# A four-layer graph network on one core: more row gathers by TensorE and SyncE in three stages

## The chip, the cores and the metric

The kernel runs on one core of one Trainium2 chip. The metric is the device time of one execution in microseconds (us).

## The reference

A graph has 12,500 nodes with 64 features and 400,000 edges, sorted by target `dst`. Four layers follow each other, each ending in x = layernorm(x + layer(x)).

```python
# layer 0: max over a node's incoming edges of W2 relu(W1 [x_dst, x_src - x_dst])
# layer 1: mean of edge_attr over a node's outgoing edges, then a two-layer network on [x, mean, u]
# layer 2: mean of x[src] over incoming edges, a gate of three groups, a linear map
msg_sum = segment_sum(feature[src], dst)
h = msg_sum / max(deg, 1)
# layer 3: attention over incoming edges; weights by type of node (4) and of edge (8), 4 heads of 16
k, q, v = (typed_linear(x, W, node_type) for W in (Wk, Wq, Wv))
a = (typed_head(k[src], rel_att, etype) * typed_head(q[dst], rel_att, etype)).sum(-1) * pri / 4
m = typed_head(v[src], rel_msg, etype)
h = segment_sum(m * softmax_over_dst(a), dst)
out = typed_linear(h, Wa, node_type)
```

## The kernel before, in words

Edges lie on chip as 128 lanes (partitions) of 3125 consecutive edges. A *tile* is one edge of each lane, so 128 rows; a *group* is 25 tiles. There are 124 such groups, and the last 25 tiles are cut into three short groups of 16, 8 and 1. Nodes are 98 tiles of 128. The program is unrolled and runs stage after stage: sorting of places, the scatter of layer 1's rows by source (L768), layers 0 and 1 over edges, a node stage, layer 2 over edges, a node stage, layer 3 over edges, a node stage.

Rows that depend on an index are fetched by GpSimd, one indirect DMA a tile (`gather`, L214): in layer 2 rows of 64 from X2 into `gx`, in layer 3 rows of 128 (keys and values, worked out in the node stage for each of 8 edge types) from TKM into `gk`. The scatter writes rows of 65 from `at` to SRT in the same way.

Some tiles are fetched otherwise. `row_by_row` (L237 to L245) loads 32 addresses into registers and issues one small DMA a row, from SyncE (SP) or ScalarE (ACT): two tiles in two groups of five in layer 2 (`ROWS2`), one tile in every third group (`single`) of layer 3 (`ROWS3`). In layer 2 two tiles a group (`PE2`) come from TensorE: x is on chip as three bf16 parts (`part`). The source number is split into a block (`key_b`) and a place among 13 x 128 columns (`keys`). A matmul spreads the keys over partitions (`pk`, L1208), DVE compares them with `own` to get a one-hot `hot` of 128 x 1664 (L1212), and 39 matmuls (13 chunks by three parts, 128 x 512, the last chunk's three 128 x 128) give the rows of eight blocks in `pr` (L1218). `take` picks the right block by `hb`, a multiply `one` (L1230) and a sum (L1231).

Each group then needs a running sum or maximum along the lane. Layer 2 has a chain of 25 scalar_tensor_tensor instructions (L1251). A layer-3 step spreads q along the lane (`st`, 25 instructions, L1419), multiplies it with the keys in five pieces and adds up (`pr`, `sc`, L1426, L1427), takes a running maximum `M` (L1434), differences `ex`, exponentials on ACT (L1442, L1443), a running denominator `L` (L1446), the weighted values `wm` (four pieces, L1454) and one long scan `hs` (L1459). ACT copies `hs`, `M` and `L` into `R`, which SP stores.

Queues: a DMA issued by SP stands in program order behind what SP issued before. In layer 3 SP's order is written out by hand, and that of the other engines is a scheduler's; in the scatter and in layer 2 SP, ACT, PE and DVE are ordered by hand. `gk` and `st` have three buffers, `gx` five, `at` four, `pr` of layer 2 four.

Of the kernel before, what the change touches and what calls it, by code (L numbers as in the profile page):

```python
# [9 lines left out]
F32 = mybir.dt.float32  # L10
BF = mybir.dt.bfloat16
# [8 lines left out]
P = 128  # L20
D = 64
# [23 lines left out]
ROWS2 = 5, (1, 3)  # L45
PE2 = 2
NC = 13
ROWS3 = 3
RL = 32
ZC = 200  # L50


@with_exitstack
def resnorm_gnn_kernel(ctx: ExitStack, tc: tile.TileContext, a: dict, out: bass.AP):
# [21 lines left out]

    const = ctx.enter_context(tc.tile_pool(name="const", bufs=1))
    to_l2 = ExitStack()
    to_l0 = ExitStack()
# [304 lines left out]

    xs = const.tile([P, NT, D], F32, name="xs")
    if NREM:
# [285 lines left out]
    def turned(k):  # L672

        if k >= len(rounds):
            return
        m, w = rounds[k][2], work[k]
        oh, ol = w["hots"]
        pT = ups.tile([NT, 4, P], F32, name="pT")
        for j in range(m):
            nc.tensor.matmul(pT[:, j, :], oh[:, j, :], identh, start=True, stop=True)  # L680
        pH = ups.tile([NT, 2, P], F32, name="pH")
        for s, n in ((0, min(2, m)), (1, m)):
            for j in range(n):
                nc.tensor.matmul(pH[:, s, :], oh[:, j, :], ol[:, j, :], start=(j == 0), stop=(j == n - 1))
        w["hT"] = hT = up.tile([NT, 4, P], HF, name="hT", bufs=3)
        nc.scalar.activation(hT[:, :m, :], pT[:, :m, :], AF.Copy)
        H = up.tile([NT, P], F32, name="H", bufs=3)
        nc.vector.tensor_add(H, now[0], pH[:, 1, :])
        now[0] = H
        if m > 2:  # L690

            w["then"] = B = up.tile([NT, P], HF, name="then", bufs=3)
            nc.vector.scalar_tensor_tensor(B, pH[:, 0, :], 1.0 / U8, w["tables"][1], op0=ALU.mult, op1=ALU.add)
# [46 lines left out]
    now = [begin]  # L740
    todo = [0]

    def advance():

        k = todo[0]
        hot(k + 2)
        turned(k + 1)
        ol = work[k]["hots"][1]
        pG = spots(k)
        if k + 2 in work:  # L750
            work[k + 2]["tables"] = tables(now[0])
        pairs(k + 1)
        sums_of(k, pG, ol)
        todo[0] += 1

# [8 lines left out]
    def scatter(i, between=()):  # L764
        at, _, to = placed.pop(i)
        for j in range(G):

# [7 lines left out]
            if j % 4 == 0 and between:  # L775
# [3 lines left out]
                puts0.append(row)  # L779
        return put  # L780

# [64 lines left out]
    keep = const.tile([P, EP], F32, name="keep")  # L846
    negm = const.tile([P, EP], F32, name="negm")
    w64 = const.tile([D, P], F32, name="w64")
# [81 lines left out]
    def carry_over(psp, sb, last):  # L930

        ps = psp.tile([D, P], F32, name="ps_c")
        nc.tensor.transpose(ps, last, ident)  # L933
        return ps
# [208 lines left out]
    to_n1.close()  # L1143


    with tc.tile_pool(name="e2", bufs=2) as sb, tc.tile_pool(name="e2ps", bufs=1, space=PSUM) as psp:
        pm = sb.tile([P, D], F32, name="m2", bufs=1)
# [5 lines left out]
        for k, g in enumerate(single):  # L1153
            at = groups[g][0] + G - 2
            nc.vector.tensor_copy(cols[:, k, :], srcS[:, at : at + 2])
        places = places_of(psp, sb, cols.rearrange("p k t -> p (k t)"), 4 * D, "places")
        at, n3 = groups[3][0] + G - 1, len(range(3, NG - 1, ROWS3))
        assert n3 <= P
        places3 = places_of(psp, const, stS[:, at : at + (n3 - 1) * ROWS3 * G + 1 : ROWS3 * G], 8 * D, "places3")
        X2b = bytes_of(X2)  # L1160
# [10 lines left out]
        for b in range(NBA):  # L1171
            t = slice(b * NB, (b + 1) * NB)
            rest = xs[:, t, :]
            for k in range(3):
                nc.scalar.activation(parts[k][:, t, :], rest, AF.Copy)
                if k < 2:
                    left = sb.tile([P, NB, D], F32, name=f"left{k}")
                    nc.vector.tensor_sub(left, rest, parts[k][:, t, :])
                    rest = left
        own = sb.tile([P, NC], F32, name="own", bufs=1)  # L1180
        nc.vector.tensor_scalar(own, frow[:, :NC], float(P), pcol, op0=ALU.mult, op1=ALU.add)
        by_pe = slice(G - 2 - PE2, G - 2)
        dense = range(2, NG - 1)
        n = len(dense) * PE2
        keys = sb.tile([P, n], HF, name="keys", bufs=1)
# [3 lines left out]
        with tc.tile_pool(name="e2k", bufs=1) as ksb:  # L1189
            num = ksb.tile([P, n], I32, name="num")  # L1190
            at = groups[dense[0]][0]
            nc.vector.tensor_copy(num.rearrange("p (g t) -> p g t", t=PE2),
                                  srcS[:, at : at + len(dense) * G].rearrange("p (g t) -> p g t", t=G)[:, :, by_pe])
            part_i = ksb.tile([P, 3, n], I32, name="part_i")
# [6 lines left out]

        def by_one_hots(g):


            k = (g - dense[0]) * PE2
            pk = psp.tile([P, PE2, P], F32, name="pk", bufs=1)
            for j in range(PE2):
                nc.tensor.matmul(pk[:, j, :], keys[:, k + j : k + j + 1].to_broadcast([P, P]), identh, start=True, stop=True)  # L1208
            got = []
            for j in range(PE2):  # L1210
                hot = sb.tile([P, NC, P], BF, name="hot", bufs=4)
                nc.vector.tensor_tensor(hot, pk[:, j, None, :].to_broadcast([P, NC, P]),  # L1212
                                        own[:, :, None].to_broadcast([P, NC, P]), ALU.is_equal)
                pr = psp.tile([P, 8, D], F32, name="pr", bufs=4)
                for c in range(NC):
# [5 lines left out]
                got.append(pr)  # L1221
            return k, got

        def take(got, gx):
            k, got = got
            for j, pr in enumerate(got):
                hb = sb.tile([P, 8], F32, name="hb", bufs=4)
                nc.vector.tensor_scalar(hb, eight, key_b[:, k + j : k + j + 1], None, op0=ALU.is_equal)
                one = sb.tile([P, 8, D], F32, name="one")
                nc.vector.tensor_mul(one, pr, hb[:, :, None].to_broadcast([P, 8, D]))  # L1230
                nc.vector.tensor_reduce(gx[:, by_pe.start + j, :], one.rearrange("p b f -> p f b"), AX.X, ALU.add)  # L1231

        ahead = {}
        with tc.manual_schedule(engines={SP, ACT, mybir.EngineType.PE, mybir.EngineType.DVE}):
            for g, (c0, ng) in enumerate(groups):
                if g + 2 in dense:
                    ahead[g + 2] = by_one_hots(g + 2)
                if g + 2 in single:
# [4 lines left out]
                gx = tiles_of(g)  # L1243
                if g in ahead:
                    take(ahead.pop(g), gx)
                mine = [j for j in range(ng) if not (g in single and j >= G - 2 or g in dense and by_pe.start <= j < by_pe.stop)]
                for j in mine:
# [8 lines left out]
        row = ends_of_lanes(sb, R2, D)  # L1256
        ps = carry_over(psp, sb, pm)
        u = sb.tile([D, P], F32, name="u2", bufs=1)
        nc.vector.tensor_tensor_scan(u, w64, ps, 0.0, ALU.mult, ALU.add)
        nc.vector.tensor_add(row, row, shifted(psp, sb, u, "g2"))  # L1260
        put_ends(R2, row)

    to_l2.close()

    def types_of(t, t0, nt):
# [24 lines left out]
    with tc.tile_pool(name="n2", bufs=1) as sb, tc.tile_pool(name="n2ps", bufs=2, space=PSUM) as psp:  # L1290
        puts = []

        def nodes2(b, t0, nt):
# [65 lines left out]
            for j in range(nt):  # L1359
# [18 lines left out]
                )  # L1378
                yield

        in_turn(nodes2, [1, 2, 4] + [NB] * (NBA - 1), lambda n: n + 1,
                {getattr(mybir.EngineType, e) for e in ('PE', 'Activation', 'DVE', 'SP')})


    with tc.tile_pool(name="e3", bufs=2) as sb, tc.tile_pool(name="e3ps", bufs=1, space=PSUM) as psp:
        pa = sb.tile([P, D], F32, name="a3", bufs=1)
# [25 lines left out]
        def step(g, c0, ng):  # L1412
            nonlocal pa, M, L, hs, last, R
            gk, st = keys_of(g), sts.pop(g)
            for j in range(ng - (g in single)):
                gather(gk[:, j, :], TKM, stS[:, c0 + j : c0 + j + 1])
            for j in range(ng):
# [5 lines left out]
            for q in range(0, ng, 5):  # L1423
# [4 lines left out]
                                        pr.rearrange("p c (h d) -> p c h d", d=HS), AX.X, ALU.add)  # L1428
            nm = negm[:, c0 : c0 + ng]
            Mp, Lp, hp = M, L, hs  # L1430
# [9 lines left out]

            weight = psp.tile([P, NH, ng], F32, name="weight", bufs=2)
            nc.scalar.activation(weight, ex[:, 1, :, 1:], AF.Exp)  # L1442
# [33 lines left out]
        R = None  # L1476
        with tc.manual_schedule(engines={SP}):
            load_starts(0)
            load_starts(1)
            for g, (c0, ng) in enumerate(groups):  # L1480
                step(g, c0, ng)

        row = ends_of_lanes(sb, R3, W3)
# [42 lines left out]
    with tc.tile_pool(name="n3", bufs=1) as sb, tc.tile_pool(name="n3ps", bufs=2, space=PSUM) as psp:  # L1526
        def nodes3(b, t0, nt):
# [28 lines left out]
            y = tile_of([P, nt, D], "y")  # L1556
            nc.vector.tensor_add(y, po, xs[:, cols, :])
            o = tile_of([P, nt, D], "o")
# [38 lines left out]
```

## Time and profile before

| what | us |
|---|---|
| median of 3 runs (lowest, highest) | 16245.76 (16243.42, 16247.37) |
| profiled execution | 16243.81 |
| its span | 16242.0 |
| GpSimd busy | 12210.0 |
| DVE busy | 10664.7 |
| PE busy | 7545.9 |
| ACT busy | 2681.6 |
| scatter, first to last indirect write (L768) | 1266.7 to 5379.7 |
| layer 2, first to last gather | 8409.2 to 11892.6 |
| layer 3, first to last gather | 12191.5 to 16056.8 |

Busy time says what an engine did, not what it waited for. GpSimd's busy time leaves out the issue of its DMAs, about 0.3 us after each. A view by stretch gives busy times, the granted TensorE clock (1.00 is full) and the DMA share of any interval; the timeline gives single instructions with the idle time before them and what ended it. Line numbers in the profile are those of the kernel before.

### The profile page before, as it was taken

Reading aid. Unit: us, or ns where it says so; the run is one execution under the profiler, and the core shown is the slowest. Engines: PE = TensorE matmul, PEld = TensorE weight load, DVE = VectorE, ACT = ScalarE, POOL = GpSimd, SP = SyncE. Lnnn points to the kernel's source line nnn. Section 1 sums busy time; section 2 is a strip of 40 time slices with the busy share of each in tenths; the row PEclk is TensorE's granted clock in tenths of the full one; section 3 lists DMA queues with packets and bytes.
Section 4 is the critical chain, followed back from the end, with each engine's and each line's share of the span. In section 5 each row is a group of like instructions: output and inputs, shape, how many; then the busy total and the mean of one; then the engine's idle time right before and its main releaser. Section 6 shows DMA issues by size and latency. Waiting matters only on the chain. (4 is left out here: it accounts for less than half of the span.)

```text
span 16242.0 us, 201759 instructions
## 1 busy us (share of the span) xinstructions
PE 7545.9 (46%) x52153; PEld 5379.1 (33%) x52153; DVE 10664.7 (66%) x29306; ACT 2681.6 (17%) x5002; POOL 12210.0 (75%) x12724
## 2 busy tenths in 40 slices
PE   4455666666654566666546666666660000000002
PEld 4444555554543455555522222222240000000002
DVE  9996777777774577777445555555545666666666
ACT  0012333333322011111120000000031212212222
POOL 7777777777777777777767777777767777777776
PEclk6667777777776677777768888888885555555555
DMA  3333233222222465656312222222253333333333
GB/s 78 120 107 90 84 86 86 69 52 54 54 52 52 154 206 195 203 200 205 114 41 56 58 59 56 57 58 59 58 180 110 109 109 109 113 106 111 112 109 97
DMA packets 1130450, 1634.82 MB, mean 101 GB/s; under 512 B 755218, under 2 KB 760850, under 8 KB 1128898
## 3 DMA queue, kind: packets, MB, share of 16 engines
q1 hardware_dynamic: 684322, 1093.23, 20.1%
q0 software_dynamic: 406880, 520.58, 13.1%
q10 hardware_dynamic: 38080, 8.06, 0.2%
q8 instruction: 414, 6.78, 0.2%
q14 instruction: 754, 6.18, 0.1%
HBM read 883.71 MB, written 737.15 MB: 100 GB/s over the span
## 5 line engine op out<-in xcount | busy, mean ns | idle before, releaser
L768 POOL DMA_INDIRECT SRT<-at,to x3125 | 3036.9, 972 | 952.5 <-issue 946.7
L214 POOL DMA_INDIRECT gk<-TKM,stS x3084 | 2926.2, 949 | 940.3 <-issue 922.3
L214 POOL DMA_INDIRECT gx<-X,srcS x2783 | 2635.2, 947 | 875.3 <-issue 791.0
L1218 PE MATMUL pr<-part,hot 128*128 128x512 bf16 (+1 forms) x9516 | 2229.7, 401 | 1176.0 <-DVE one L1230 1150.1
L214 POOL DMA_INDIRECT gb<-TB,srcS x2125 | 2073.1, 976 | 647.6 <-issue 624.5
L1251 DVE SCALAR_TENSOR_TENSOR gx<-gx,keep 128x64 f32<-128x64 f32 x3124 | 892.6, 286 | 1463.2 <-DMA gx<-X,srcS 1226.7
L933 PE MATMUL ps_c<-ident,full 128*64 128x128 f32 x3 | 1.3, 420 | 3900.4 <-DVE full L1486 3898.9
L1218 PEld LDWEIGHTS <-hot 128*128 128x128 bf16 x9516 | 975.2, 105 | 2430.5 <-DVE hot L1212 858.0
L1066 DVE SCALAR_TENSOR_TENSOR R<-R,negm,msg 128x64 f32<-128x64 f32 x3124 | 858.0, 275 | 820.5 <-PE msg L997 816.2
L933 PEld LDWEIGHTS ps_c<-ident,full 128*64 128x64 f32 x3 | 0.4, 128 | 3901.8 <-DVE full L1486 3899.7
L214 POOL DMA_INDIRECT xg<-in_x,srcS x1000 | 953.6, 954 | 306.2 <-issue 296.6
L1426 DVE TENSOR_TENSOR pr<-st,gk 128x320 f32<-128x320 f32 x627 | 306.8, 490 | 1135.3 <-DMA gk<-TKM,stS 1110.3
L1419 DVE SCALAR_TENSOR_TENSOR st<-st,keep 128x64 f32<-128x64 f32 x3124 | 886.0, 284 | 209.1 <-DMA st<-S 114.4
L371 DVE TENSOR_TENSOR ol<-iota,lo 128x512 f16<-128x512 f32 (+2 forms) x1000 | 982.3, 982 | 0.0
L680 PE MATMUL pT<-identh,oh 128*98 128x128 f16 x3125 | 412.0, 262 | 1184.7 <-DVE oh L368 1182.7
L991 PE MATMUL pt<-ident,st 128*128 128x128 f32 (+1 forms) x3250 | 823.6, 353 | 213.5 <-DVE st L1057 196.0
L1057 DVE SCALAR_TENSOR_TENSOR st<-st,keep 128x64 f32<-128x64 f32 x3124 | 869.4, 278 | 1.1
L728 PE MATMUL pG<-ol,mb 128*128 128x128 f16 x4625 | 768.2, 240 | 196.7 <-ACT mb L712 195.5
L990 PE MATMUL pt<-ident,gb 128*128 128x128 f32 (+1 forms) x2210 | 574.3, 354 | 590.4 <-DMA gb<-TB,srcS 584.3
L1025 DVE SCALAR_TENSOR_TENSOR r<-r,keep 128x64 f32<-128x64 f32 x3000 | 836.0, 279 | 0.0
L368 DVE TENSOR_TENSOR oh<-iota,hi 128x392 f16<-128x392 f32 (+2 forms) x1000 | 787.3, 787 | 24.0 <-SPq L509 23.8
L728 PE MATMUL pG<-A,hT 98*128 98x128 f16 x3125 | 726.5, 242 | 0.0
(350 smaller groups left out, 19284.9 us busy)
## 6 DMA issues: line engine op xcount, KB each, us to landing
st<-S SPq DMA_DIRECT2D x248, 800.0 KB
R<-R SPq DMA_DIRECT2D x124, 900.0 KB
r<-SRT SPq DMA_DIRECT2D x125, 812.5 KB
R<-r SPq DMA_DIRECT2D x125, 812.5 KB
gx<-X ACTq DMA_DIRECT2D x6272, 0.2 KB
gx<-X SPq DMA_DIRECT2D x6272, 0.2 KB
S<-zero SPq DMA_DIRECT2D x200, 500.0 KB
R<-R SPq DMA_DIRECT2D x124, 800.0 KB
```

The source lines that it names most:

```text
L214: return nc.gpsimd.indirect_dma_start(out=to, out_offset=None, in_=table, in_offset=bass.IndirectOffsetOnAxis(ap=at, axis=0))
L368: nc.vector.tensor_tensor(oh, iota[:, None, :NT].to_broadcast([P, n, NT]), hi[:, :, None].to_broadcast([P, n, NT]), ALU.is_equal)
L371: nc.vector.tensor_tensor(ol, iota[:, None, :].to_broadcast([P, n, P]), lo[:, :, None].to_broadcast([P, n, P]), ALU.is_equal)
L728: nc.tensor.matmul(pG[:, j, :], l, r, start=(n == 0), stop=(n == len(terms) - 1))
L768: put = nc.gpsimd.indirect_dma_start(out=SRT, out_offset=bass.IndirectOffsetOnAxis(ap=to[:, j : j + 1], axis=0), in_=at[:, j, :], in_offse ...
L991: nc.tensor.matmul(pt[:w, k, :], two_tiles(st, k, w), ident, start=False, stop=True)
L1025: nc.vector.scalar_tensor_tensor(r1[:, j, :D], pm1, keep1[:, c : c + 1], r1[:, j, :D], op0=ALU.mult, op1=ALU.add)
L1057: nc.vector.scalar_tensor_tensor(st[:, j, :], pa, keep[:, c : c + 1], st[:, j, :], op0=ALU.mult, op1=ALU.add)
L1066: nc.vector.scalar_tensor_tensor(R[:, j, :], pm, negm[:, c : c + 1], msg[:, j - q, :], op0=ALU.add, op1=ALU.max)
L1218: nc.tensor.matmul(pr[:, :m, :].rearrange("p b f -> p (b f)"), hot[:, c, :], parts[part][:, 8 * c : 8 * c + m, :].rearrange("p b f -> p (b ...
L1251: nc.vector.scalar_tensor_tensor(gx[:, j, :], pm, keep[:, c : c + 1], gx[:, j, :], op0=ALU.mult, op1=ALU.add)
L1419: nc.vector.scalar_tensor_tensor(st[:, j, :], pa, keep[:, c : c + 1], st[:, j, :], op0=ALU.mult, op1=ALU.add)
```

## The change

It has three parts. In the scatter, in 35 groups (every third from 3 on) one tile is written row by row by SP. In layer 2, odd groups get three tiles from TensorE and even ones two, from group 3 on; the one-hots are made a group earlier than the products, and `pr` gets seven PSUM buffers. In layer 3, tile 22 of every group from 3 to 123 comes from TensorE: x after layer 2 is kept as three bf16 parts (`x3`, made in the node stage) with a table of node types; one-hot products give x and the type, a transpose and the weights by type give key and value, a product with the edge-type weights gives all eight, and a mask (`only`) with eight matmuls by the identity (`sum_of`) picks one. PE's order in layer 3 is now by hand. For room, fp32 `xs` ends before layer 3 (the last node stage adds up `x3`), and layer 3 recomputes `nm` in each group.

```diff
-PE2 = 2
+PE2 = 2, 3
+ROWS1 = 3
...
+    single1 = range(ROWS1, HISTG - ROWS1, ROWS1)
...
+            nc.tensor.transpose(work[k + 1]["pH"][:1, 2, :], placed[g][1][:, G - 1 :], ident)
+            in_a_row[g] = up.tile([1, P], I32, name="in_a_row", bufs=AHEAD + 2)
+            nc.vector.tensor_scalar(in_a_row[g], work[k + 1]["pH"][:1, 2, :], U8, None, op0=ALU.mult)
...
-        for j in range(G):
+        for j in range(G - (i in single1)):
...
+        for p in range(0, P, RL):
+            _, spots_ = nc.values_load_multi_w_load_instructions(
+                in_a_row[i][:, p : p + RL], engines=[mybir.EngineType.SP], min_val=0, max_val=E - 1,
...
+            for r, spot in enumerate(spots_):
+                put = nc.sync.dma_start(SRT[ds(spot, 1), :], at[p + r : p + r + 1, G - 1, :])
...
-        dense = range(2, NG - 1)
+        dense = range(3, NG - 1)
+        def by_pe(g):
+            return range(G - 2 - PE2[g % 2], G - 2) if g in dense else ()
...
-                pr = psp.tile([P, 8, D], F32, name="pr", bufs=4)
+                pr = psp.tile([P, 8, D], F32, name="pr", bufs=7)
...
             for g, (c0, ng) in enumerate(groups):
+                if g + 3 in dense:
+                    hots[g + 3] = one_hots_of(g + 3)
                 if g + 2 in dense:
-                    ahead[g + 2] = by_one_hots(g + 2)
+                    ahead[g + 2] = products(hots.pop(g + 2))
...
+    x3 = [parts3.tile([P, NT, D], BF, name=f"x3_{k}") for k in range(3)]
+    ntab = parts3.tile([P, NT], BF, name="ntab")
...
+            in_parts(lambda shape, name: tile_of(shape, name, 1), xs, x3, cols)
...
+        nc.sync.dma_start(types[:, :NFULL], of[: NFULL * P].rearrange("(t p) -> p t", p=P))
...
+        def only(rows, hot8):
+            one = sb.tile([P, 8, D], F32, name="one", bufs=3)
+            nc.vector.tensor_mul(one, rows, hot8[:, :, None].to_broadcast([P, 8, D]))
+            return one
+        def sum_of(to, one):
+            for b in range(8):
+                nc.tensor.matmul(to, ident, one[:, b, :], start=(b == 0), stop=(b == 7))
+        def one_hot_3(g):
+            k = g - dense[0]
+            nc.tensor.matmul(pk, keys[:, k : k + 1].to_broadcast([P, P]), identh, start=True, stop=True)
+            hots[g] = hot = sb.tile([P, NC, P], BF, name="hot", bufs=2)
+            nc.vector.tensor_tensor(hot, pk[:, None, :].to_broadcast([P, NC, P]),
+                                    own[:, :, None].to_broadcast([P, NC, P]), ALU.is_equal)
+        def products_3(g):
+            hot = hots.pop(g)
+            of_x[g] = pr = psp.tile([P, 8, D], F32, name="big", bufs=2)
+            for c in range(NC):
+                m = min(8, NT - 8 * c)
+                for part in range(3):
+                    nc.tensor.matmul(pr[:, :m, :].rearrange("p b f -> p (b f)"), hot[:, c, :],
+                                     x3[part][:, 8 * c : 8 * c + m, :].rearrange("p b f -> p (b f)"),
+                                     start=(c == 0 and part == 0), stop=(c == NC - 1 and part == 2))
+            for c in range(NC):
+                m = min(8, NT - 8 * c)
+                nc.tensor.matmul(p8[:, :m], hot[:, c, :], ntab[:, 8 * c : 8 * c + m], start=(c == 0), stop=(c == NC - 1))
+        def take_3(g):
+            k, pr = g - dense[0], of_x.pop(g)
+            hb = sb.tile([P, 8], F32, name="hb")
+            nc.vector.tensor_scalar(hb, frow[:, :8], key_b[:, 0, k : k + 1], None, op0=ALU.is_equal)
+            sum_of(x1, only(pr, hb))
+            t8 = sb.tile([P, 8], F32, name="t8")
+            nc.vector.tensor_mul(t8, p8, hb)
+            ty = sb.tile([P, 1], F32, name="ty")
+            nc.vector.tensor_reduce(ty, t8, AX.X, ALU.add)
+            ht = sb.tile([P, NTY], F32, name="ht")
+            nc.vector.tensor_scalar(ht, frow[:, :NTY], ty, None, op0=ALU.is_equal)
+            by_types[g] = bt = sb.tile([P, NTY, D], F32, name="bt")
+            nc.vector.tensor_mul(bt, x1[:, None, :].to_broadcast([P, NTY, D]), ht[:, :, None].to_broadcast([P, NTY, D]))
+        def keys_and_values(g):
+            bt = by_types.pop(g)
+            for k in range(2):
+                nc.tensor.transpose(tT[:, k * P : (k + 1) * P], bt[:, 2 * k : 2 * k + 2, :].rearrange("p t f -> p (t f)"), ident)
+            tTs = sb.tile([P, 2 * P], F32, name="tTs", bufs=1)
+            nc.scalar.activation(tTs, tT, AF.Copy)
+            for k in range(2):
+                nc.tensor.matmul(kvT, wkqv[:, k, 0:2, :].rearrange("p s f -> p (s f)"), tTs[:, k * P : (k + 1) * P],
+                                 start=(k == 0), stop=(k == 1))
+            kvTs = sb.tile([P, P], F32, name="kvTs", bufs=1)
+            nc.scalar.activation(kvTs, kvT, AF.Copy)
+            he = sb.tile([P, ETY], F32, name="he")
...
+            for w in range(2):
+                of = slice(w * D, (w + 1) * D)
+                pw = psp.tile([P, ETY, D], F32, name="big", bufs=2)
+                nc.tensor.matmul(pw.rearrange("p e f -> p (e f)"), kvTs[of], wkm[of].rearrange("p e f -> p (e f)"),
+                                 start=True, stop=True)
+                chosen[g].append(only(pw, he))
+        def put_keys_and_values(g):
+            for w, one in enumerate(chosen.pop(g)):
+                sum_of(kv1[:, w * D : (w + 1) * D], one)
+            nc.scalar.activation(keys_of(g)[:, by_pe, :], kv1, AF.Copy)
...
-            nm = negm[:, c0 : c0 + ng]
+            nm = sb.tile([P, ng], F32, name="nm")
+            nc.vector.tensor_scalar(nm, keep[:, c0 : c0 + ng], -NEG, NEG, op0=ALU.mult, op1=ALU.add)
...
-        with tc.manual_schedule(engines={SP}):
+        with tc.manual_schedule(engines={SP, mybir.EngineType.PE}):
...
             for g, (c0, ng) in enumerate(groups):
+                if g + 3 in dense:
+                    one_hot_3(g + 3)
+                if g + 1 in dense:
+                    keys_and_values(g + 1)
+                if g + 2 in dense:
+                    products_3(g + 2)
+                if g + 1 in dense:
+                    put_keys_and_values(g + 1)
                 step(g, c0, ng)
+                if g + 2 in dense:
+                    take_3(g + 2)
...
-            nc.vector.tensor_add(y, po, xs[:, cols, :])
+            nc.vector.tensor_add(y, x3[0][:, cols, :], x3[1][:, cols, :])
+            nc.vector.tensor_add(y, y, x3[2][:, cols, :])
+            nc.vector.tensor_add(y, y, po)
```

## The prediction, made before the changed kernel was run

> **What bounds the kernel now.** I read the profile's table of costly groups and its chain first, then busy time by stretch, then the timeline of single groups in layers 2 and 3.
>
> ```profile
> POOL 18%; issue 6%; DMA 1%; DVE 1%; PE 1%; ACT 0%; SPq 0%; POOLq 0%; DVEq 0%; ACTq 0%
> L768 POOL DMA_INDIRECT SRT<-at,to x3125 | 3036.9, 972 | 952.5 <-issue 946.7
> L214 POOL DMA_INDIRECT gk<-TKM,stS x3084 | 2926.2, 949 | 940.3 <-issue 922.3
> L214 POOL DMA_INDIRECT gx<-X,srcS x2783 | 2635.2, 947 | 875.3 <-issue 791.0
> ```
>
> GpSimd waits for nothing but its own issue in the three stages that the change touches; it is the clock there. From first to last of these instructions: scatter 1266.7 to 5379.7 us with 3125 + 98 of them, 1.276 us each; layer 2 8409 to 11893, 2783, 1.252 us; layer 3 12191.5 to 16056.8, 3084, 1.2534 us. A layer-3 group costs 24.67 x 1.2534 = 30.9 us.
>
> ```profile
> 8500.00:10500.00 2000.00, 1321.74 (x5760) 583.54 (x5760) 1037.80 (x2379) 0.00 (x0) 1512.11 (x1599) 0.81 0.22 57
> 12500.00:15500.00 3000.00, 0.00 (x0) 0.00 (x0) 1951.48 (x5161) 614.67 (x684) 2270.59 (x2393) 0.50 0.36 110
> 16128.00:16242.00 114.00, 94.40 (x410) 86.66 (x409) 82.28 (x193) 34.33 (x90) 69.66 (x72) 0.50 0.37 84
> 9007.50:9013.00 5.50, 5.42 (x13) 1.93 (x13) 5.06 (x13) 0.00 (x0) 4.04 (x5) 0.50 0.13 27
> 9013.00:9026.50 13.50, 13.39 (x68) 6.19 (x66) 2.92 (x11) 0.00 (x0) 10.16 (x11) 1.00 0.15 28
> 9026.50:9030.00 3.50, 0.00 (x0) 0.00 (x0) 1.35 (x5) 0.00 (x0) 2.83 (x3) 1.00 0.16 32
> 9030.00:9031.00 1.00, 0.00 (x0) 0.00 (x0) 0.36 (x2) 0.00 (x0) 0.70 (x1) 0.53 0.14 28
> ```
>
> Columns: stretch, length, busy time of PE, weight loads, DVE, ACT, POOL, granted TensorE clock, DMA share, GB/s. In layer 2 PE is 66% busy and in layer 3 it is silent. A layer-2 burst of 78 products starts at half clock (13 in 5.5 us, 0.427 us each), rises to 1.00 after 5.5 us (0.197 us each), and 3.6 us after it ends the clock is 0.5 again. The last stage is 83% PE-busy with narrow fp32 matmuls and never leaves 0.50.
>
> ```profile
> 13525.36 0.26 ACT L1442 ACTIVATE weight<-ex 128x100 f32<-128x100 f32 x1
> 13525.65 0.83 DVE L1454 TENSOR_TENSOR wm<-gk,weight 128x400 f32<-128x400 f32 x1
> 13529.43 3.62 DVE L1459 TENSOR_TENSOR_SCAN hs<-dec,wm 128x1664 f32<-128x1664 f32 x1
> 13532.98 1.86 DVE L1419 SCALAR_TENSOR_TENSOR st<-st,keep 128x64 f32<-128x64 f32 x6
> ...
> 9002.98 3.68 DVE L1212 TENSOR_TENSOR hot<-pk,own 128x1664 bf16<-128x1664 f32 x2
> ...
> 12079.81 3.07 PE L1353 MATMUL po<-wkqv,tT 128*128 128x64 f32 x26
> ...
> 16134.55 1.75 PE L1284 MATMUL ps_t<-ident,two 128*128 128x128 f32 x7 [1.34 <-ACT two L1277]
> 16137.00 6.47 PE L1553 MATMUL po<-wa,tT 128*128 128x64 f32 x28 [0.70 <-DVE tT L1286]
> ```
>
> When the gathers are there, DVE does one layer-3 group in 20.2 us (hs at 13529.43, the next at 13549.61), of which 7.33 from the first `wm` to the end of `hs` and 11.3 on the 25 `st` and five `pr`/`sc` pairs. An fp32 matmul of 64 columns (two records each) takes 0.22 us at the fast clock (14 in 3.07) and 0.46 at the slow one (14 in 6.47).
>
> **Scatter.** 35 groups give one tile to SyncE: 35 x 1.276 = -44.7 us on POOL. SP gets 128 row writes every third group. A layer-3 row read costs 0.366 us on that queue (64 in 23.42), so 47 us of the 95 that three groups take. The rows stand behind the next `at` load and ahead of the one after, so the load into this group's buffer comes some 18 us late, every third time. DVE waits for it at L666, but works two groups ahead of POOL (63 us), so POOL does not feel it. A write may cost more than a read; POOL would be reached near 0.75 us a row. Between 0 and -44.7 I take -44.7.
>
> **Layer 2.** Tiles by TensorE: 122 x 2 = 244 before, 61 x 3 + 60 x 2 = 303 after: 59 gathers less, 59 x 1.252 = -73.9 us. PE per two groups: 5 x 39 x 0.197 = 38.4, and two slow starts of 13 x 0.23 = 6, so 44.4 of the 54 us that POOL needs. The products now start a step after their one-hots, and seven PSUM buffers replace four, so the wait on `one` (682 us of PE in 2000) shrinks. DVE gains half a tile a group (0.5 x 3.8 us on 14.4 of 27). SP and ACT rows there take 0.5 us each, 63 of the 68 us that 2.5 groups will take: still under. -70.
>
> **Layer 3, POOL alone:** 121 gathers x 1.2534 = -151.7 us, 29.7 us a group. This needs everything new to fit below 29.7. DVE: hot 1.88, three `one` at 0.69, seven small ones at about 0.2, `bt` (bounds: a small one's 0.23 and `one`'s 0.69; I take 0.43, half the width): +5.8, so 26 of 29.7. PE about 20. As sums they fit.
>
> **Layer 3, as a chain.** The built order shows that they stand in one ring. `bt` comes after `hs`; from it PE transposes, ACT copies, PE forms kvT, ACT copies, PE forms two `pw`. The products for g+2 wait, by PE's order, for both `pw`, and for DVE to empty the first by `one`, since `big` has two buffers. After the products come p8 and 16 sums for g+1. ACT's copy of these into `gk` stands ahead of the exponentials of step g, and `wm` waits for both. Then `hs`, and round again: once per group, nothing overlaps. From the end of `hs`:
> - `bt`: hot 1.88, bt 0.43, four small links: at 3.1.
> - two transposes at 0.25 (L1284, slow clock), copy 0.38, two kvT at 0.46, copy 0.3, and `pw` at 1.15 (0.59 in layer 2's node stage at clock 0.94, doubled for the slow one), five hand-overs of 0.05 and a drain: first `pw` at 7.0, second at 8.1.
> - 39 products: 7.7 at full clock, +0.23 for each slow one. Six slow, as two `pw` run just ahead: 9.1. To 17.3.
> - p8, 13 narrow ones at 0.1 (scatter's 128-column matmuls: 701.5 us for 7105 at 2400 to 3500): 1.3.
> - 16 sums: 3.5 fast, 7.4 slow; the clock falls 3.6 us after wide work ends, so 4.0.
> - copy 0.3, exponential 0.26, hand-overs 0.15, then 7.33.
> Sum 30.7, already over 29.7. DVE's order repeats every three steps; in two of them this holds. In the third (g = 6, 9, ...; the scheduler thought `st` late) `one` of the new products stands ahead of nearly all of `st`, `pr`, `sc`: DVE idles until 17.4 and only then does 0.7 + 11.0 + 1.6 + 7.33 = 38.1. Mean (30.7 + 30.8 + 38.1) / 3 = 33.2 us a group against 30.9.
>
> Time of the stage: step 1 ends near 12267; 120 ringed steps x 33.2 = 3984; two full groups at 20.2 and three short ones of 28 together: last `hs` at 16319 against 16084 now: +235 us. POOL, needing 29.7, runs ahead and waits for `gk`.
>
> **A rule against it.** The trace's burst was slow for 5.5 us after idling and fell back 3.6 us after its end. The Trainium skill, "TensorE: Matmul & The Clock Gate", "HAM oscillation — how this bites in real kernels", says that idle gaps over about 3.4 us make every burst start slow again. Here DVE's 10 us from `wm` to `bt` leave such a gap in each ring. By the rule's 3.4 us, eight products are slow (9.5 us); by the row, 13 (10.7). I stay at 9.1 because `pw` precedes; the row's number would add 1.6 us a group, +190 us.
>
> **Node stages.** x3 adds three ACT copies (0.54, 128x448) and two DVE subtractions a block; PE there waits for ACT's `km` already: 13 x 1 us, bounds 0 and 21. The transposed load of node types: "DMA: Bandwidth & Descriptors", "Rules for kernel authors", says a strided last dimension makes a descriptor per element, 12,500 here; no row shows it. Layer 2's 256-byte rows take 33 ns of an engine (0.22 x 16 engines over 106 rows a us): 26 us if nothing hides it; estimate +7. The last stage gets two more DVE adds of 0.6 a block, beside a PE that bounds it: +5. `nm` (0.2 us a group) lies in ring slack, or in the third step: in the rounding.
>
> **Sum**, on the profiled execution's 16243.8 (span 16242.0): -44.7 - 70 + 235 + 20 + 5 = 16389; the median of the runs, 16245.8, is 2 above it. About 16390 us.
>
> **Rivals.**
> 1. GpSimd stays the bound, and it is faster. The place is layer 3's ring: at 29.7 us or less the time is 16243.8 - 44.7 - 70 - 151.7 + 25 = 16002; the sign turns at a mean of 31.5. With all products fast (7.7) and fast sums (3.5) the mean is 31.6 or a little less. For it: engine sums fit. Against: the third step's serial 11 us alone.
> 2. TensorE stays slow: 13 slow products, sums at 6, p8 at 2: 35.0 and 39.7, mean 36.6: another 120 x 3.4 = 408, so 16800. For it: the last stage at 0.50.
> 3. SyncE's row writes hold the scatter: 0 there, 16435. Against: half the queue is free.
>
> **How the numbers follow.** Ring as laid out, 16280 to 16640: 0.62. Slow clock beyond: 0.12. Rival 3 inside the main range: 0.05. Ring so short that the parts cancel: 0.07. Rival 1 or the way to it: 0.14. A difference of 0.2% (32 us) is about what a measurement of this kernel can tell. Slower 0.79, same 0.07, faster 0.14. The range 16200 to 16660 takes in all of the first, third and fourth case, the near half of the slow clock and the fringe of rival 1; it leaves out about 0.11 below and 0.07 above.
>
> **What would show it.** `hs` every 33 us in a pattern of two short and one long; POOL idle for `gk`'s release, DVE waiting for PE at `one` and for ACT or PE at `wm`; granted clock between 0.6 and 0.85; scatter shorter by 45, layer 2 by 70. Wrong if POOL still issues every 1.25 us through layer 3.

## The result and the profile after

The changed kernel takes 16595.8 us (median of four runs, 16594.3 to 16604.2) against 16244.6 us for the kernel before: 351 us more, a ratio of 1.0216 with a 95% interval of 1.0203 to 1.0229. The profiled execution has a span of 16602.3 us, 360 above that of before.

These lines of the page after (the chain's shares, then the costliest groups: count, busy, mean ns, idle before and its releaser) answer to the first four shown of before:

```profile
PE 6%; DVE 5%; SPq 1%; issue 1%; ACT 0%; POOL 0%; DMA 0%; DVEq 0%; ACTq 0%; POOLq 0%
L217 POOL DMA_INDIRECT gk<-TKM,stS x2963 | 2835.4, 957 | 1410.0 <-issue 1373.3
L782 POOL DMA_INDIRECT SRT<-at,to x3090 | 3003.8, 972 | 942.3 <-issue 905.4
L217 POOL DMA_INDIRECT gx<-X,srcS x2724 | 2585.3, 949 | 930.7 <-issue 786.0
```

GpSimd has left the chain that ended last (18% before, 0% now), and TensorE and DVE share it. The `gk` gathers are 121 fewer, yet GpSimd's idle time among them grew from 940 to 1410 us: it now waits where it used to set the pace. The row names no releaser ("issue"), but the timeline does: between 12500 and 15500 us it has 29 pauses of some 11 us among its gathers, one every three groups, and each ends 0.8 to 1.1 us after the end of a group's last `wm`, the last reader of a `gk` buffer. The `gx` gathers are 59 fewer: 50 us less busy, 55 us more idle.

By stretch (length; busy PE, weight loads, DVE, ACT, POOL; granted clock, DMA share, GB/s), layer 2 and layer 3:

```profile
8500.00:10500.00 2000.00, 1516.06 (x7189) 691.62 (x7188) 1168.15 (x2521) 0.00 (x0) 1489.85 (x1574) 0.87 0.23 57
12500.00:15500.00 3000.00, 1960.99 (x9767) 1193.62 (x9765) 2060.97 (x5595) 636.67 (x879) 1995.11 (x2084) 0.67 0.33 98
```

In layer 3 no engine is busy for more than 69% of the time (GpSimd's issue, 0.3 us a gather, comes on top of its 66%), which is how a ring of waits looks. Scatter and layer 2 below go from the first to the last indirect DMA of the stage, the last stage from the last `wm` to the end:

| stage | before, us | after, us | change | predicted |
|---|---|---|---|---|
| scatter | 4113.0 | 4069.7 | -43 | -45 |
| layer 2 | 3483.4 | 3488.7 | +5 | -70 |
| layer 2's last gather to layer 3's first | 298.9 | 307.3 | +8 | +20 |
| layer 3, first gather to last `wm` | 3891 | 4271 | +380 | +235 |
| last stage | 159 | 167 | +8 | +5 |

One group of layer 3, from the timeline after (start, length, engine, line, operation, in brackets the idle time before it and what ended it):

```profile
14009.96 3.62 DVE L1625 TENSOR_TENSOR_SCAN hs<-dec,wm 128x1664 f32<-128x1664 f32 x1
14010.00 3.65 PE L1484 MATMUL bank<-one,ident 128*128 128x64 f32 x16 [4.46 <-DVE wm L1620]
...
14016.19 0.42 DVE L1520 TENSOR_TENSOR bt<-bank,ht 128x256 f32<-128x256 f32 x1
14016.66 0.69 PE L1526 MATMUL bank<-ident,bt 128*128 128x128 f32 x2 [2.91 <-DVE bt L1520]
14017.82 1.22 PE L1530 MATMUL bank<-tTs,wkqv 128*128 128x128 f32 x4 [0.47 <-ACT tTs L1528]
14019.41 2.08 PE L1540 MATMUL big<-wkm,kvTs 64*128 64x512 f32 x4 [0.37 <-ACT kvTs L1533]
14021.52 0.69 DVE L1479 TENSOR_TENSOR one<-big,he 128x512 f32<-128x512 f32 x1 [0.51 <-PE big L1540]
14022.26 10.54 PE L1500 MATMUL big<-x,hot 128*128 128x512 bf16 x39 [0.78 <-DVE one L1479]
14032.64 0.47 PE L1505 MATMUL bank<-ntab,hot 128*128 128x8 bf16 x13
14032.97 3.77 PE L1484 MATMUL bank<-one,ident 128*128 128x64 f32 x32
14036.77 0.28 ACT L1547 ACTIVATE gk<-bank 128x128 f32<-128x128 f32 x1 [9.50 <-PE bank L1484]
14037.08 0.26 ACT L1608 ACTIVATE bank<-ex 128x100 f32<-128x100 f32 x1
14037.36 0.83 DVE L1620 TENSOR_TENSOR wm<-gk,bank 128x400 f32<-128x400 f32 x1 [3.84 <-ACT bank L1608]
14041.15 3.62 DVE L1625 TENSOR_TENSOR_SCAN hs<-dec,wm 128x1664 f32<-128x1664 f32 x1
```

Read it downwards: from `bt` on, each instruction starts when the one above it ends (ACT's two short copies, `tTs` and `kvTs`, fill the gaps of 0.47 and 0.37 us). The copy into `gk` on ACT is for the next group, but the exponential of this group (L1608) stands behind it, and `wm` waits for that. `hs` to `hs` is 31.2 us. Every third group is longer, because `one` of the new products stands ahead of nearly all `st`:

```profile
14053.33 10.37 PE L1500 MATMUL big<-x,hot 128*128 128x512 bf16 x39 [0.78 <-DVE one L1479]
14063.73 0.69 DVE L1479 TENSOR_TENSOR one<-big,hb 128x512 f32<-128x512 f32 x1 [9.41 <-PE big L1500]
14064.34 1.56 DVE L1584 SCALAR_TENSOR_TENSOR st<-st,keep 128x64 f32<-128x64 f32 x5
...
14080.71 3.62 DVE L1625 TENSOR_TENSOR_SCAN hs<-dec,wm 128x1664 f32<-128x1664 f32 x1
```

DVE stands still for 9.4 us and only then does its 16 us of `st` to `wm`: 39.6 us. Through the stage the steps repeat as 31.7, 31.2, 39.6.

### The profile page after: what moved, and what is told of

It reads as the page before. It is cut to its first block, busy times and chain, and to the rows that moved or that the text cites. A ratio compares the mean times of both kernels' runs of the same rounds, so it can differ in the third digit from the quotient of the medians.

```text
span 16602.3 us, 249780 instructions
## 1 busy us (share of the span) xinstructions
PE 10549.4 (64%) x67979; PEld 7196.1 (43%) x67979; DVE 11340.6 (68%) x30989; ACT 2816.6 (17%) x5413; POOL 12043.8 (73%) x12509
## 5 line engine op out<-in xcount | busy, mean ns | idle before, releaser
L217 POOL DMA_INDIRECT gk<-TKM,stS x2963 | 2835.4, 957 | 1410.0 <-issue 1373.3
L217 POOL DMA_INDIRECT gx<-X,srcS x2724 | 2585.3, 949 | 930.7 <-issue 786.0
L1262 PE MATMUL pr<-part,hot 128*128 128x512 bf16 (+1 forms) x11817 | 2544.5, 378 | 494.9 <-DVE one L1274 485.7
L1262 PEld LDWEIGHTS <-hot 128*128 128x128 bf16 x11817 | 1153.5, 100 | 1879.0 <-issue 658.2
L1484 PE MATMUL bank<-one,ident 128*128 128x64 f32 x5808 | 900.0, 326 | 933.1 <-DVE wm L1620 932.3
L1500 PE MATMUL big<-x,hot 128*128 128x512 bf16 (+1 forms) x4719 | 1282.1, 443 | 108.3 <-DVE one L1479 108.3
L1484 PEld LDWEIGHTS bank<-one,ident 128*128 128x128 f32 x5808 | 866.7, 239 | 947.6 <-issue 945.3
L1500 PEld LDWEIGHTS <-hot 128*128 128x128 bf16 x4719 | 528.5, 113 | 1032.0 <-issue 691.7
L683 PEld LDWEIGHTS <-oh 128*98 128x98 f16 x3125 | 290.3, 152 | 1250.2 <-DVE oh L371 1246.2
```

Source lines behind the costliest of these rows:

```text
L217: return nc.gpsimd.indirect_dma_start(out=to, out_offset=None, in_=table, in_offset=bass.IndirectOffsetOnAxis(ap=at, axis=0))
L1262: nc.tensor.matmul(pr[:, :m, :].rearrange("p b f -> p (b f)"), hot[:, c, :], parts[part][:, 8 * c : 8 * c + m, :].rearrange("p b f -> p (b ...
L1484: nc.tensor.matmul(to, ident, one[:, b, :], start=(b == 0), stop=(b == 7))
L1500: nc.tensor.matmul(pr[:, :m, :].rearrange("p b f -> p (b f)"), hot[:, c, :], x3[part][:, 8 * c : 8 * c + m, :].rearrange("p b f -> p (b f) ...
```

## The experiments

All runs beside the kernel before of their own chips (16246.7, 16252.8 and 16251.8 us for the three sets of runs); layers 2 and 3 are the times from first to last gather in the profiled execution (before: 3483.4 and 3865.3, the changed kernel: 3488.7 and 4244.1). The sets are l3_off, one_part, in_order and rows2_early; pipelined, pipelined_link, warm and pipelined_early; l2_two, rows_half and pe3.

| run | median, us | ratio to before (95%) | layer 2 | layer 3 |
|---|---|---|---|---|
| l3_off | 16210.2 | 0.9977 (0.9968 to 0.9986) | 3476.6 | 3867.3 |
| one_part | 16075.1 | 0.9897 (0.9881 to 0.9914) | 3477.2 | 3726.0 |
| in_order | 16685.1 | 1.0270 (1.0253 to 1.0287) | 3481.1 | 4333.4 |
| pipelined | 16086.3 | 0.9899 (0.9882 to 0.9915) | 3457.7 | 3756.5 |
| pipelined_link | 16371.2 | 1.0073 (1.0056 to 1.0090) | 3459.1 | 4036.3 |
| warm | 16127.9 | 0.9923 (0.9906 to 0.9939) | 3459.5 | 3794.9 |
| rows2_early | 16553.3 | 1.0188 (1.0171 to 1.0205) | 3447.1 | 4244.2 |
| l2_two | 16219.9 | 0.9981 (0.9971 to 0.9990) | 3492.2 | |
| rows_half | 16215.5 | 0.9977 (0.9968 to 0.9987) | 3484.4 | |
| pipelined_early | 16039.0 | 0.9868 (0.9851 to 0.9884) | 3428.2 | 3749.5 |
| pe3 | 16102.2 | 0.9903 (0.9887 to 0.9920) | 3471.8 | |

Kernels with the same layer 2 as the changed one take 3477 to 3481 us there in the first set, 3458 to 3460 in the second, and the changed kernel 3489. So layer 2 is best compared within a set, where it repeats to some 5 us; across sets it differs by up to 30, and the whole time with it.

**Is it layer 3 alone? (l3_off)**

```diff
         hots, of_x, by_types, chosen = {}, {}, {}, {}
+        dense = range(0)
```

> The changed kernel with layer 3's TensorE tile given back to GpSimd (all 121 tiles gathered again); the bf16 parts of x, the node types on chip and the changed layer 2 and scatter stay. Ring theory (all of layer 3's loss is the ring of DVE, TensorE and ACT that the tile builds): layer 3 from its first gather to its last wm goes from 4271 us back to 3891, and the whole from 16596 to about 16216, some 28 below the kernel before. Rival (part of the loss lies in the new tables, in SBUF space or in the earlier stages): over 16240.

16210.2 us, and layer 3's gathers take 3867.3 us, 2 more than before. The whole loss sits in layer 3's tile; the rest of the change gains 36 us.

**Are the products a link of the chain? (one_part)**

```diff
-                for part in range(3):
+                for part in range(1):
```

> Leaves out part of the computation: layer 3's products use one of the three bf16 parts of x, 13 products in place of 39; order and everything else as in the changed kernel. Ring theory (the products are a link of the chain in every group): 26 fast products at 0.197 us are 5.1 us a group less, which takes the mean of 34.4 to GpSimd's 29.7, so about 120 x 4.6 = 550 us less, near 16045. Rival (the products lie beside DVE's work, DVE or the copy order sets the step): less than 100 us off, over 16490.

521 us less, 518 of it in layer 3. Many steps now go 27.2, 26.7 and 34.8 us, 4.5 to 4.8 less each, as far as GpSimd lets them: nearly all that the products give up, the step gives up.

**A written order, first try (in_order)**

```diff
-        with tc.manual_schedule(engines={SP, mybir.EngineType.PE}):
+        with tc.manual_schedule(engines={SP, ACT, mybir.EngineType.PE, mybir.EngineType.DVE}):
...
                 pa = st[:, j, :]
+            if g + 1 in dense:
+                choose_3(g + 1)
+            if g + 2 in dense:
+                products_3(g + 2)
...
+            if g + 2 in dense:
+                sum_x_3(g + 2)
             hs = sb.tile([P, D, ng + 1], F32, name="hs")
...
             nc.sync.dma_start(lanes(R3)[:, c0 : c0 + ng, :], R)
+            if g + 2 in dense:
+                take_3(g + 2)
+            if g + 1 in dense:
+                put_keys_and_values(g + 1)
```

Here `choose_3` is the two `one` of `pw`, `sum_x_3` the `one` of the products, p8 and x's sums; the calls at the head of the loop go, but for `one_hot_3` and `keys_and_values`.

> The changed kernel with layer 3's DVE and ACT in an order written out (hot, all st, the two one of pw, pr and sc, M, ex, wm, one of the products, hs, then bt), the products put after pw as before, and the node-type products, the sums and ACT's copy into gk put behind wm. Same instructions. Ring theory (only the order makes the ring; DVE has 26 us and TensorE 22 to 26 us of work a group, GpSimd 29.7): layer 3 runs at GpSimd's 29.7 us a group, 3891 - 145 = 3746 us in place of 4271; the whole about 16070, under the kernel before. Rival (the work on TensorE at a slow clock, or on DVE, is too much in any order): layer 3 stays over 4100 us, the whole over 16430.

A miss: 89 us slower than the changed kernel, all of it in layer 3 (34.9 us a group). The timeline of in_order names what I had built in:

```profile
14006.59 7.09 PE L1484 MATMUL bank<-one,ident 128*128 128x64 f32 x32 [1.46 <-DVE bt L1531]
14013.47 0.31 PE L1488 MATMUL bank<-identh,keys 128*128 128x128 f16 x1
14013.82 1.89 DVE L1490 TENSOR_TENSOR hot<-bank,own 128x1664 bf16<-128x1664 f32 x1 [7.29 <-PE bank L1488]
```

The sums of keys and values lie in one PSUM tile (`bank2` in the kernel) with x's sums, and they waited for `bt`, which reads that tile; the granted clock was 0.50 through them and they took 7.1 us in place of 3.8. `pk` stands behind them on TensorE, and `hot`, the head of DVE's step, waited 7.3 us for it. One ring had been opened and another closed. The theory was not refuted by this, but nor was it supported.

**The same instructions without either ring (pipelined), and one link put back (pipelined_link)**

```diff
+                if q == 10:
+                    if g + 1 in dense:
+                        choose_3(g + 1)
+                    if g + 2 in dense:
+                        row_3(g + 2)
+                        products_3(g + 2)
...
+            if g + 2 in dense:
+                one = only(of_x.pop(g + 2), hbs[g + 2])
+            if g + 1 in dense:
+                put_keys_and_values(g + 1)
+            if g + 2 in dense:
+                node_types_3(g + 2)
+                sum_of(x1, one)
             hs = sb.tile([P, D, ng + 1], F32, name="hs")
...
+            if g + 1 in dense:
+                copy_keys_and_values(g + 1)
+            nc.scalar.activation(R[:, :, :D], hs[:, :, 1:].rearrange("p f c -> p c f"), AF.Copy)
...
+            if g + 3 in dense:
+                one_hot_3(g + 3)
+            if g + 2 in dense:
+                take_3(g + 2)
```

`pk` alone stays ahead, behind `pw`; `hot` (`one_hot_3`) now follows `hs`. pipelined_link moves two of these calls up:

```diff
+            if g + 1 in dense:
+                put_keys_and_values(g + 1)
+                copy_keys_and_values(g + 1)
             weight = weights[g % 2][:, :, :ng]
             nc.scalar.activation(weight, ex[:, 1, :, 1:], AF.Exp)
```

> The changed kernel with layer 3 in another written order, which mends what held the order of in_order back (there DVE's hot stood first in the step and waited for TensorE's pk, which stood behind 16 slow sums that waited for bt). Now st, pr and sc are interleaved, the two one of pw follow the third chunk, products come after them, the kv sums directly behind the products, then p8 and the sums of x, hot behind hs, ACT's copy into gk behind the exponentials and dec. Same instructions. Ring theory: DVE has about 26 us a group, TensorE 22 to 25, so GpSimd's 29.7 us rules again: layer 3 takes about 3746 us in place of 4271, the whole about 16070. Rival (the work is too much for DVE or TensorE in any order): over 31 us a group, over 16300.

> pipelined with one link of the ring put back: the 16 sums of keys and values and ACT's copy of them into gk for the next group stand ahead of this step's exponentials, as in the changed kernel. Ring theory: the exponentials then wait for products (end at 18 us of the step), sums (3.8) and copy, wm, one, hs, hot and bt follow in DVE's order: 32.8 us a group in place of 29.7, so about 370 us more than pipelined, near 16440. Rival (that copy has slack, other parts of the order made the loss): within 60 us of pipelined.

pipelined takes 16086.3 us, 510 less than the changed kernel (488 of it in layer 3) and 1% under the kernel before: the same work fits once it is in another order. Its row of the `gk` gathers and its stretch of layer 3:

```profile
L217 POOL DMA_INDIRECT gk<-TKM,stS x2963 | 2817.1, 951 | 940.7 <-issue 891.4
12500.00:15500.00 3000.00, 2291.49 (x10977) 1511.63 (x11076) 2425.72 (x6377) 689.31 (x997) 2253.75 (x2371) 0.69 0.35 111
```

GpSimd's idle time is back to 941 us and its 2371 gathers at 1.252 us fill 2968 of the 3000 us, so it sets the pace again. DVE is 81% busy in place of 69%, and the clock is hardly higher (0.69): this gain owes little to the clock. With the one link back the time is 285 us more (370 expected), and steps go 31.8 and 33.0 us (32.8 expected). That link, ACT's copy for the next group ahead of this group's exponentials (TensorE's order is the same in both), is thus enough by itself to make the kernel slower than before.

**What does the slow clock cost? (warm)**

```diff
+            def warm(n):
+                for _ in range(n):
+                    nc.tensor.matmul(pw0.rearrange("p e f -> p (e f)"), x3[0][:, 0:2, :].rearrange("p b f -> p (b f)"),
+                                     x3[0][:, 0:8, :].rearrange("p b f -> p (b f)"), start=True, stop=True)
+
+            warm(8)
             for k in range(2):
...
             nc.scalar.activation(tTs, tT, AF.Copy)
+            warm(2)
...
                                  start=(k == 0), stop=(k == 1))
+            warm(2)
             kvTs = sb.tile([P, P], F32, name="kvTs", bufs=1)
```

`pw0` is the buffer that the first `pw` fills.

> The changed kernel with 12 wide bf16 products more in each group of layer 3, whose output pw overwrites: 8 ahead of the two transposes, 2 ahead of kvT's and 2 ahead of pw's wait for ACT. Clock theory (products start slow because only narrow or short work precedes them; wide work in the gap lifts the clock first): pw 1.0 us less, products 7.7 us in place of 10.5, sums 0.3 less, against about 1.6 us of delay by the added ones: 2.5 us a group less, 300 in all, near 16300, granted clock of the stage from 0.67 to over 0.85. Rival (the first dozen products are slow for another reason, as the load of weights or PSUM's release): 1.6 us a group more, near 16790.

468 us less (449 of it in layer 3), more than forecast: twelve products of no use in each group bring the changed kernel under the kernel before. From its timeline and its stretch of layer 3:

```profile
14005.17 0.44 PE L1534 MATMUL bank<-ident,bt 128*128 128x128 f32 x2
14006.08 0.71 PE L1539 MATMUL bank<-tTs,wkqv 128*128 128x128 f32 x4
14007.15 1.13 PE L1550 MATMUL big<-wkm,kvTs 64*128 64x512 f32 x4
14009.06 8.10 PE L1500 MATMUL big<-x,hot 128*128 128x512 bf16 x38 [0.78 <-DVE one L1479]
12500.00:15500.00 3000.00, 2147.81 (x11964) 1369.68 (x12160) 2328.73 (x6326) 719.25 (x989) 2237.43 (x2346) 0.80 0.35 110
```

Every link on TensorE is shorter, not only the products: 0.25 us in the transposes, 0.5 in kvT, 1.0 in `pw`, 2.4 in the products. Steps go 27.5, 27.4 and 36.4 us, 3.7 less on average, and 121 x 3.7 = 450 is the change of layer 3 (4244.1 to 3794.9). I had not expected the delay of 1.6 us that the added products could bring to lie almost wholly in waits that were there already.

**Where did layer 2's 59 gathers go? (rows2_early, l2_two, rows_half)**

rows2_early:

```diff
-                gxs[g] = sb.tile([P, groups[g][1], D], F32, name="gx", bufs=5)
+                gxs[g] = sb.tile([P, groups[g][1], D], F32, name="gx", bufs=6)
...
-                if g + 2 in single:
-                    to, k = tiles_of(g + 2), 2 * single.index(g + 2)
+                if g + 3 in single:
+                    to, k = tiles_of(g + 3), 2 * single.index(g + 3)
```

l2_two and rows_half, both on l3_off:

```diff
-PE2 = 2, 3
+PE2 = 2, 2
```
```diff
-ROWS2 = 5, (1, 3)
+ROWS2 = 5, (1,)
```

> The changed kernel with layer 2's row-by-row tiles asked for three groups ahead in place of two (six gx buffers, six hot buffers in place of seven). Theory 1 (the queue of single rows on SyncE and ACT bounds layer 2, because it stands still for each R2 write while the rows themselves need only 130 of the 136 us that five groups take on GpSimd): first to last gather of layer 2 goes from 3489 to about 2724 x 1.252 = 3410 us, the whole from 16596 to about 16517. Rival (TensorE's products or DVE hold the groups, or the rows themselves are too slow): no change within 15 us.

> l3_off with layer 2's tiles by TensorE back to two in every group (244 in place of 303, 59 gathers more on GpSimd), so that layer 2's new share is undone while its new order, the scatter and the tables stay. Row-queue theory (single rows on SyncE and ACT hold layer 2 near 3480 us whatever GpSimd sheds): 2785 gathers x 1.252 = 3486 us, 10 more than l3_off's 3476.6, the whole within 20 of 16210. Rival (the third tile brings what it takes off GpSimd): 74 more, near 16284.

> l3_off with single rows in one group of five in layer 2 in place of two, so 48 to 50 gathers more on GpSimd and half the rows on SyncE and ACT. Row-queue theory: with half the rows the queue is free and GpSimd runs at its own rate, 2773 gathers x 1.252 = 3472 us, no more than l3_off's 3476.6; the whole within 20 of 16210, and DVE's wait for rows (565 us in 2000) gone. Rival (rows are not the bound, they only relieve GpSimd): 62 more, near 16272.

l2_two, with 61 gathers more than l3_off, is 31.9 us under the kernel before of its own chip; rows_half, with 50 gathers more and half of the single rows, 36.3; l3_off was 36.5 under. So neither relief of GpSimd is worth more than 5 us here, and half of the rows can go for nothing. rows2_early gains 43 of the 79 us, which neither theory said. What DVE waited for in 2000 us of layer 2 (us in total, times, longest), before, after, and in rows_half:

```profile
DVE gx L1251 <- DMA gx<-X,srcS: 679.7, 737, 2.9
DVE gx L1251 <- DMA gx<-X: 109.8, 15, 10.9
```
```profile
DVE gx L1298 <- DMA gx<-X: 565.4, 24, 37.7
DVE gx L1298 <- DMA gx<-X,srcS: 199.6, 218, 2.4
```
```profile
DVE gx L1298 <- DMA gx<-X,srcS: 775.7, 573, 19.3
```

`gx<-X` are the single rows, `gx<-X,srcS` GpSimd's gathers. Before, DVE waited mostly for GpSimd. After the change it waits 24 times for rows, 24 us each; with half the rows it never does and waits for GpSimd alone.

The rows on ACT in the whole trace, before and after, and those on SyncE in l3_off and rows2_early, which are of one set of runs (count, ns of one issue, first and last start):

```profile
L245 ACTq DMA_DIRECT2D gx<-X x6272: 234/234/1070, 8422.0 to 11827.1; - x196
```
```profile
L248 ACTq DMA_DIRECT2D gx<-X x6272: 234/235/1076, 8380.6 to 11807.2; - x196
```
```profile
L248 SPq DMA_DIRECT2D gx<-X x6272: 227/228/442, 8416.0 to 11842.3; - x196
L248 SPq DMA_DIRECT2D gx<-X x6272: 227/228/355, 8375.6 to 11812.5; - x196
```

ACT's come every 0.543 us before and 0.546 after, so 256 of them in five groups are 139 and 140 us. A queue that only kept step with the stage would show the same average, so its waits decide: in the 2000 us after the change SyncE's rows waited 360 us for earlier single rows to land and never for a buffer. So this is the queue's own pace. It already was as slow as GpSimd before the change (111 x 1.252 = 139 us); with GpSimd down to 136 it is the bound.

Asking a group earlier left that pace as it was: SyncE's rows take 3426 us from first to last in l3_off and 3437 in rows2_early. It gave them a head start: the first row leaves 6 us after the first gather in place of 46, and layer 2 is 29.5 us shorter than in l3_off, as pipelined_early's is than pipelined's. The head start is used up along the stage: in rows2_early DVE does not wait for rows at all from 8500 to 9300 us, then 36 and 110 us in the next two stretches of 800, and 171 us in the 900 after them.

**Both mends together (pipelined_early), and more for TensorE (pe3)**

pe3 is pipelined_early with

```diff
-PE2 = 2, 3
+PE2 = 3, 3
```

> pipelined and rows2_early together (layer 3 in the new order, layer 2's single rows asked for three groups ahead). If the two losses are independent, pipelined less 43: about 16027, 220 under the kernel before. Rival (they share a resource, as SyncE's queue): less than 20 us under pipelined.

> pipelined_early with three tiles by TensorE in every group of layer 2 (364 in place of 303). GpSimd sheds another 61 x 1.252 = 76 us, to 106 gathers in five groups, 133 us, against 130 us of single rows on SyncE and ACT; TensorE has 117 products, 23 us and at times a slow start, in 26.6. If rows and TensorE just fit: 40 to 70 less, near 15980. Rival (the rows' queue, which has 3 us in 133 to spare, holds it): within 20 of pipelined_early's 16039.

pipelined_early is the fastest version: 16039.0 us, 557 under the changed kernel and 1.3% under the kernel before. The two gains add: it is 47 us under pipelined, where rows2_early was 43 under the changed kernel. pe3 is 63 us slower than it, which neither expectation said. Its layer 2 is 44 us longer with 60 gathers fewer, and a part of that can be the chips', as the two are not of one set. In 2000 us of it DVE waits 253 us for gathers, 243 for `pk` from a TensorE that is 90% busy, and 105 for rows; which of these costs the time was not tried apart.

## Why the prediction was wrong in size

The direction and the mechanism held, the sum did not: +351 measured, +145 predicted. By its steps:

- **Scatter, -44.7: right** (-43). A row write cost 0.47 us (128 in 60.0), not the 0.366 of a row read, but the point at which it would reach GpSimd was 0.75.
- **Layer 2, -70: failed, +5.** The step was "SP and ACT rows there take 0.5 us each, 63 of the 68 us that 2.5 groups will take: still under". ACT's row takes 0.543 us over the whole stage of the trace of before, so 128 of them are 69.5 us and not under, and after the change DVE waits for them. The forecast margin was 8%, and the 0.5 was low by as much: a close race between two queues asks for the count and the first and last start of the whole stage. The other parts of that step (TensorE's time, `one`'s wait, DVE) do not show among DVE's waits after the change.
- **Layer 3, +235: right mechanism, mis-sized by 145.** 116 of that is the group: 120 steps took 4100 us, 34.2 each, against 3984, 33.2 each. In a short step the products start 8.7 us after `hs` ends (predicted 8.1) and take 10.5 in place of 9.1, p8 0.5 in place of 1.3, the sums 3.8 in place of 4.0, and copy to `hs` 8.0 as predicted. The long step is 39.6 in place of 38.1, for the same reason. 28 is the start: "step 1 ends near 12267" put it 75.5 us behind the first gather; it is 104 in the trace of before as well as after, and I had not looked.
- **The clock: the wrong side of the two was chosen.** The trace of before had 13 slow products in a burst; I took six, because `pw` runs just ahead. 11 to 14 were slow in 116 of the 121 groups, 12 on average. `pw`, two transposes and kvT, with gaps of 0.4 to 2.9 us, did not lift the clock: in the group shown it is granted at 0.50 until 14027.2 us, 5.0 us after the products began. In warm, with the gap ahead of the transposes filled, it rises 5.6 us after the sums ahead of it began, and hardly a product is slow. The Trainium skill's rule on idle gaps ("TensorE: Matmul & The Clock Gate", "HAM oscillation — how this bites in real kernels") pointed the right way; taking its 3.4 us for the length of the slow start too makes eight slow (an estimate), and the trace's number was the better one. The cost was also undervalued: I priced products alone (190 us), while warm, in the group shown, has `pw`, kvT and transposes together 1.7 us shorter as well.
- **Node stage, +20, and last stage, +5:** +8 each.
- **A slip in the sums:** rival 1 has the sign turn at a mean of 31.5 us. From the sum itself it is 32.0, 145 / 120 = 1.2 us under 33.2.

Of the rivals, the first is what pipelined is: GpSimd the bound at 29.7 us a group, 16002 predicted. With layer 2's 70 not there it is 16072, and pipelined measured 16086, in steps of 30.1 us. The order of the instructions (the scheduler's on DVE and ACT, the written one on TensorE), not the idea of the change, made it slower. Rival 2 (13 slow products and slow sums, 16800) had the products right, but the sums follow them at once and are fast. Rival 3 did not occur.

## What to carry to other kernels

Before giving an idle engine part of a loop, follow the loop once round: an instruction that waits holds up what stands behind it in its engine's order, as ACT's copy held up the exponential here, and such a ring can be slower than the busiest engine alone, though every sum of work per engine fits. Where a written or scheduled order puts the next group's result ahead of this group's instructions on any engine, move it behind; here it took no more instructions and decided the sign. And when the leading engine is relieved, compare every other queue's own total for the stage, from its first to its last instruction, with the new pace, not with the old one, and see from its waits whether that total is its own.

## What the runs showed of the hardware

- Useless work can pay: twelve wide products in each of 121 groups took 468 us off. They fill TensorE's gaps, its clock rises ahead of the work that counts (0.80 granted in place of 0.67 in the same 3000 us), and in 119 of the groups no product is slow any more.
- A 128x8 bf16 product takes 0.036 us (13 in 0.47) right behind wide ones, a third of what I had put down.
- Single-row DMAs came at different paces: 0.366 us for reads on SP alone in layer 3, 0.47 us for writes on SP in the scatter, and 0.54 us on ACT while SP issues rows as well. What of this is the queue's, the direction's or the company's was not tried apart.
- A queue of single rows can bound a stage by its own pace: an earlier start then shifts it (40 us of head start, 29.5 us of gain) and does not speed it up.
